# A graph layer on one core: another split of the gathered rows between two DMA queues, and one transfer for two groups

## The chip, the core and the metric

The kernel runs on one core of a Trainium2 chip. A core has a matrix engine (TensorE, PE in the profile), a vector engine (VectorE, DVE), an activation engine (ScalarE, ACT), a general engine (GpSimd, POOL) and a small engine that only waits and issues (SyncE, SP). DMA transfers are issued by SyncE, ScalarE and GpSimd and are carried out by DMA engines beside them. An issue is an instruction of the issuing engine, in order with its others; in the profile such instructions stand under SPq and ACTq and are not counted as busy time. The metric is the time of one execution in microseconds (us), as the device measures it.

## The reference

The layer has 6250 nodes with 128 features and 206250 edges, sorted by receiver. Cut to what matters:

```python
w = silu(edge_attr_32 @ rad_W1 + rad_b1) @ rad_W2 + rad_b2
w = w + silu(edge_attr_32_n2 @ sph_W1 + sph_b1) @ sph_W2 + sph_b2      # 206250 x 128
q = (x @ Wq)[receivers];  k = (x @ Wk)[senders];  v = (x @ Wv)[senders]
alpha = (q * w * k).reshape(-1, 8, 16).sum(-1) / 4 * edge_weight[:, None]
out = segment_sum(alpha[..., None] * v.reshape(-1, 8, 16), receivers, 6250) / 16
return layernorm(x + out.reshape(-1, 128))
```

## The kernel before

**Tiling.** A tile is 128 edges. Four tiles make a quad (512 edges) and four quads a group (2048 edges); there are 403 quads in 101 groups. Because the edges are sorted by receiver, the receivers of a quad lie in a window of 32 nodes.

**Startup (to about 90 us).** TensorE makes a table `kv_tab` in DRAM with k and v of every node, 1 KB a node. The receivers of all edges, relative to the start of their quad's window (`rel`), are transposed in tiles of 128 x 128 (`turn_rel`), stored to DRAM in `rel_lin` (L484) and spread from there to `rel_four`, four copies a quad (L489), so that a later load can put a quad's row of receivers on many partitions. This is done in two steps: `first_rel` for the first tile, and `store_rel(1, ...)` for the rest.

**The main loop** goes over the quads in a fixed order (in a group 0, 2, 1, 3; `slot` is the place in that order), with every instruction's place written out by hand. Iteration i does, for quads near i: on TensorE the group sums, the first layers of quad i+2 (L566), the queries at the edges of quad i+1 (L585) and its second layers (L618); on ScalarE the two silus of quad i+2 (L603) with copies between them; on GpSimd the gathers of quad i+14 from `kv_tab` (L142), one indirect DMA a tile of 128 edges; on VectorE the product of queries and keys (L634, `multiply`), the scores (L642, L644, L647) and messages (L659). The last matmul of L585 gives the one signal of TensorE in an iteration. The silus, the multiply and the next gathers wait for it.

**Row tiles.** GpSimd does not gather everything. In 58 of the quads, spread evenly (`row_at`), the fourth tile of 128 edges is fetched by 128 single DMAs of one row of 1 KB each (L212, tile `wide`); such a quad has three gathers and not four. Each row needs its address in a register. SyncE and ScalarE share these rows: ScalarE issues the last `ROW_ACT = 68`, SyncE the first 60. The registers are loaded from `at_i` by a load for up to 32 rows on SyncE and 24 on ScalarE (L206). `load_rows(i)`, at the end of each iteration, hands both engines their due part of the rows by a planner: a row costs 1, a register load `ROW_LOAD = 6`, and tile k is to be issued evenly over the 6.776 iterations that end six quads (`ROW_LEAD`) before the quad that uses it. ScalarE may put one row ahead of its copies and one behind (`next_rows` in `copies`); the rest comes behind its second silu. VectorE waits for the rows and the gathers of a quad at L631, just ahead of its multiply.

**What else SyncE issues, per group:** the node features x of a group (L315, at slot 0, for g+3), the receivers `relb` (L263, at slot 2, for g+3), the edge features `feats` (L252, at slot 3, for g+3) and the finished output (L777, at slot 1). x and feats are issued behind a wait for a signal of TensorE (`past`). SyncE works through all of it in program order.

The few lines that matter most:

```python
n = P - ROW_ACT
row_open.append({SP: rows_by(nc.sync, SP, 0, n), ACT: rows_by(nc.scalar, ACT, n, P)})
...
if slot == 3 and g + 3 < NG:
    load_feats(g + 3, past)
if slot == 2 and g + 3 < NG:
    load_rel(g + 3, lp, 4)
...
load_rows(i)
```

Of the kernel before, what the change touches and what calls it, by code (L numbers as in the profile page):

```python
# [12 lines left out]
F32 = mybir.dt.float32  # L13
BF16 = mybir.dt.bfloat16
# [7 lines left out]
SP = mybir.EngineType.SP  # L22
ACT = mybir.EngineType.Activation
WAIT = mybir.DependencyInfo(mybir.DependencyClass.Sync, mybir.DependencyReason.DATA)

P = 128
# [6 lines left out]
GT = 16  # L33
QT = 4
NQ = GT // QT
NG = math.ceil(E / (P * GT))
NT = NG * GT
EG = P * GT
EQ = P * QT
QUADS = math.ceil(E / EQ)  # L40
NB = math.ceil(N / P)
NBC = 7
ROWS = (NB + 1) * P
W = 32
# [7 lines left out]
ROW_FIRST = 8  # L52
ROW_LAST = 401
ROW_LEAD = 6
ROW_ACT = 68
ROW_AT = {SP: 0, ACT: 64}
ROW_LOAD = 6
ROW_CARRY = 2
ROW_UNITS = {SP: 32, ACT: 24}
# [14 lines left out]
def gnn_kernel(ctx, tc, x, src, dst, weight, edges, rad_W1, rad_b1, rad_W2, rad_b2,  # L74
# [14 lines left out]
    nc = tc.nc  # L89
    const = ctx.enter_context(tc.tile_pool(name="const", bufs=1))  # L90
    dram = ctx.enter_context(tc.tile_pool(name="dram", bufs=1, space=DRAM))

    kv_tab = dram.tile([NB * P, 2 * D], F32, name="kv_tab")
    rel_lin = dram.tile([NT, P], BF16, name="rel_lin")
    rel_four = dram.tile([NT // QT, NQ, EQ], BF16, name="rel_four")
    acc = dram.tile([ROWS, D], F32, name="acc")

    wkv = const.tile([P, 2 * D], F32, name="wkv")
# [29 lines left out]
    gp = ctx.enter_context(tc.tile_pool(name="group", bufs=2))  # L128
# [18 lines left out]

    order = [g * NQ + j for g in range(NG) for j in (0, 2, 1, 3) if g * NQ + j < QUADS]
    row_at = [ROW_FIRST + (n + 1) * (ROW_LAST - ROW_FIRST) // ROW_TILES for n in range(ROW_TILES)]
# [25 lines left out]
    feats_of, relb_of, act_of, kv_of, hot_of, hotT_of, x_of, q_of, msg_of = ({} for _ in range(9))  # L175
# [71 lines left out]
            return [(t, kv_of[q][:, t, :])]  # L247
        return [(slice(0, QT - 1), kv_of[q][:, :QT - 1, :]), (slice(QT - 1, QT), row_of[q])]

    def load_feats(g, mark=None):  # L250
        feats_of[g] = gp.tile([P, EG // 2], F32, name="feats", bufs=3)
        o = nc.sync.dma_start(feats_of[g], edges[g])  # L252
        if mark is not None:
            tc.add_manual_dep(o.ins, mark.ins.name, WAIT, reason="one signal of TensorE a quad")

    def quads_in(g):
        return min(NQ, QUADS - g * NQ)

    def load_rel(g, pool, bufs):

        relb_of[g] = pool.tile([P, EQ], BF16, name="relb", bufs=bufs)
        r = rel_four[g * NQ:(g + 1) * NQ].rearrange("j n e -> (j n) e")
        nc.sync.dma_start(relb_of[g], r[:, None, :].to_broadcast([NQ * NQ, W // NQ, EQ]))  # L263

    made = []

# [72 lines left out]
    with tc.tile_pool(name="nodes", bufs=1) as nodes, \  # L339
# [54 lines left out]
        relT = nodes.tile([P, math.ceil(NT / P), P], BF16, name="relT")  # L394
# [82 lines left out]
            nc.tensor.transpose(pt[:n, 0, :], rel[:, t:t + n], ident)  # L477
            nc.scalar.activation(relT[:n, t // P, :], pt[:n, 0, :], AF.Copy)

        def store_rel(a, b):  # L480
            for i, n in ((slice(a, min(b, NT // P)), P), (slice(NT // P, b), NT % P)):
                if i.start < i.stop:
                    t = slice(i.start * P, i.start * P + (i.stop - i.start) * n)
                    nc.sync.dma_start(rel_lin[t, :].rearrange("(n p) e -> p n e", p=n), relT[:n, i, :])  # L484
            a, b = a * P // QT, min(b * P, NT) // QT
            r = rel_lin.rearrange("(q t) e -> q (t e)", t=QT)
            for a, b in ((a, b - b % (P // 8)), (b - b % (P // 8), b)):
                if a < b:
                    nc.sync.dma_start(rel_four[a:b], r[a:b, None, :].to_broadcast([b - a, NQ, EQ]))  # L489

        def first_rel():
            turn_rel(0)
# [11 lines left out]
        n = len(chunks)  # L504
# [18 lines left out]
        for i, (k, n) in enumerate(work):  # L523
            if i + 2 < len(work):
                turn(*work[i + 2])
            kvs = k_and_v(k, n)
            for o, w in smalls[i:i + 1]:
                nc.scalar.dma_start(o, w)
            if i in behind:
                gather_x(behind[i], mark_of[k])  # L530
            if i >= len(chunks):
                kv_of[k[0]] = kvs
                a, b = ((j - len(chunks)) * (math.ceil(NT / P) - 1) // XQ for j in (i, i + 1))
                for t in range(a + 1, b + 1):
                    turn_rel(t * P)
                for f in beside.get(i, []):
                    f()
                continue
            store(k, kvs)
            if k + 8 < len(chunks):  # L540
                load_nodes(k + 8)
            if k == 4:
                nc.sync.dma_start(src_i, src)
            for f in beside.get(k, []):
                f()
            if i == len(chunks) - 1:
                load_rel(0, gp, 1)
                load_feats(0)
                for g in range(1, XL):
                    load_x(g)  # L550
                    load_feats(g)
                nc.sync.dma_start(scale, weight)
        for n, q in enumerate(order[XQ:AHEAD]):
            gathers(q, mark_of[quads_x[min(n + 2, XQ - 1)], "x"] if n else None)
        nc.vector.tensor_tensor(bsum, b2[:, 0:1], b2[:, 1:2], op=OP.add)
        store_rel(1, math.ceil(NT / P))
        nc.vector.tensor_scalar(scale, scale, SCALE, None, op0=OP.mult)


    with tc.tile_pool(name="ps", bufs=1, space=PSUM) as pp, tc.tile_pool(name="loop", bufs=1) as lp:  # L560
# [239 lines left out]
            nc.vector.tensor_scalar(general, found, 0.0, None, op0=OP.is_gt)  # L800

        written, ready, ready_at = [], [], []
        load_rel(1, lp, 4)
        load_rel(2, lp, 4)
        silus(order[0], first_layers(order[0]))
        pick(1)
        q_at_edges(order[0])
# [2 lines left out]
        mark = weigh(order[0])  # L810
        seen = [mark] * 3
        for g in range(NG - 1):
            for slot, j in enumerate((0, 2, 1, 3)):
                q = g * NQ + j
                i = g * NQ + slot
                turned, past, last = None, seen[-2], seen[-1]
                if slot == 0 and g == CHECK + len(checks) + 1:
                    verdict()
                if slot == 0:
                    turned = turn_q(g + 1, pp.tile([P, EQ], F32, name="pq", bufs=2))  # L820
                if slot == 1 and 2 <= g:
                    turned = sum_group(g - 2)
                if slot == 2:
                    turned = make_q(g + 1, pp.tile([P, EQ], F32, name="pq", bufs=2))
                if 1 <= g:
                    for t in ((), (0, 1), (2,), (3,))[slot]:
                        mark = sum_quads(g - 1, t)
                first_layers(order[i + 2])
                mark = q_at_edges(order[i + 1])
                seen.append(mark)  # L830
                weigh(order[i + 1])

                def copies():
                    next_rows(ACT, 1, loads=False)
                    if turned:
                        turned()
                    if 1 <= g and slot == 3:
                        part_sums(g - 1)
                    next_rows(ACT, 1, loads=False)

                silus(order[i + 2], mark, copies)
                if ready and ready_at[-1] <= i:
                    scaled(*ready.pop(0), i)
                if i + AHEAD < len(order):
                    gathers(order[i + AHEAD], last)
                multiply(order[i + 1], mark)
                messages(q, scores(q))
                if slot == 0:
                    if g + XL < NG:
                        load_x(g + XL, past)  # L850
                if slot == 3 and g + 3 < NG:
                    load_feats(g + 3, past)
                if slot == 2 and g + 3 < NG:
                    load_rel(g + 3, lp, 4)
                if slot == 0 and 1 <= g:
                    one_hots(g)
                if slot == 1:
                    one_hots_T(g + 1)
                    if g + 2 < NG:
                        pick(g + 2)  # L860
                if slot == (2 if g < NG - 2 else 0) and 1 <= g:
                    place(g - 1)
                if slot == 1:
                    write_rows(1, i)
                if slot == (3 if g < NG - 2 else 2):
                    if 2 <= g:
                        statistics(g - 2)
                if slot == 3:
                    if CHECK <= g < CHECK + len(checks):
                        checks[g - CHECK]()  # L870
                if g == NG - 4 and slot == 0:
                    place(NG - 2)
                if g == NG - 4 and slot == 1:
                    wide_one_hots(order[-1])
                if g == NG - 4 and slot == 3:
                    place(NG - 1)
                if g == NG - 3 and slot in (0, 2):
                    wide_one_hots(order[slot // 2 - 3])
                if g == NG - 2 and slot == 0:
                    n = nc.values_load(general, min_val=0, max_val=1)  # L880
                if g == NG - 3 and slot in (1, 3):
                    weigh_wide(order[slot // 2 - 3])
                if g == NG - 2 and slot == 1:
                    weigh_wide(order[-1])
                load_rows(i)
        g, (a, b, c) = NG - 1, order[-3:]
        first_layers(c)
        mark = q_at_edges(b)
# [41 lines left out]
        mark = q_at_edges(c)  # L930
# [196 lines left out]
```

## Time and profile before

| | |
|---|---|
| median of 3 runs | 2572.93 us (2570.8 to 2580.83) |
| the profiled execution's own time | 2581.4 us |
| its span (first to last instruction) | 2579.6 us |
| TensorE matmul, weight load | 2090.3 us (81%), 1743.4 us (68%) |
| VectorE, ScalarE, GpSimd busy | 1527.9 us (59%), 644.5 us (25%), 1474.3 us (57%) |
| granted TensorE clock | 0.844 |
| DMA | 307.15 MB, 119 GB/s |

The profile is one execution. In a timeline row stand the start and the length in us, the engine, the line, the operation, what it writes and reads, how many instructions are merged in the row, and in brackets how long the engine was idle before and what ended that. In the view of waits a row gives who waited at which line, for whom, the total in us, how many times, and the longest. In the view of stretches a row gives the stretch and its length in us, the busy time of an engine with the count of its instructions, and at the end the granted clock, the DMA engines' busy share and GB/s. "Remote" is a release that the profile puts down to no instruction it shows.

### The profile page before, as it was taken

The page shows a single profiled execution, that of the slowest core. Times are in us where ns is not written, and L with a number is a line of the kernel's source. Part 1 is how long each engine was busy: PE and PEld are TensorE (multiplying, and loading weights), DVE is VectorE, ACT ScalarE, POOL GpSimd, SP SyncE. Part 2 cuts the span into 40 slices and gives each one's busy share as a digit, 9 for nine tenths or more (in the row PEclk, how much of TensorE's full clock was granted, in tenths as well). Part 3 has the DMA queues.
Part 4 walks back from the last instruction along what each step waited for, and adds up shares of the span by engine and source line. Part 5 has one row for each costly group of instructions (what it writes and reads, how often), then busy time and mean ns, then how long its engine had stood idle before and what let it go on. Part 6 is the DMA issues. An engine that isn't in the chain of part 4 may idle for free.

```text
span 2579.6 us, 56198 instructions
## 1 busy us (share of the span) xinstructions
PE 2090.3 (81%) x16002; PEld 1743.4 (68%) x16002; DVE 1527.9 (59%) x3423; ACT 644.5 (25%) x1361; POOL 1474.3 (57%) x1562
## 2 busy tenths in 40 slices
PE   7687888888887878778788788888788888888788
PEld 6566766676666666667667676667566666666677
DVE  5465665656665655555556556556556555566568
ACT  2122222222222222222222222222222222222224
POOL 5565655656565556556566556556565555565550
PEclk8688888878888888888888888878888887888889
DMA  7433434344343434333343433334343443333331
GB/s 272 130 120 105 122 113 124 113 121 122 114 121 114 121 116 122 111 117 113 117 122 114 122 113 121 118 110 124 105 121 114 120 122 110 117 115 121 118 108 38
DMA packets 156799, 307.15 MB, mean 119 GB/s; under 512 B 41798, under 2 KB 90880, under 8 KB 156480
## 3 DMA queue, kind: packets, MB, share of 16 engines
q0 software_dynamic: 74080, 201.69, 27.0%
q1 hardware_dynamic: 72736, 97.22, 11.4%
q10 hardware_dynamic: 9664, 4.58, 0.7%
q8 instruction: 127, 2.08, 0.3%
q14 instruction: 192, 1.57, 0.2%
HBM read 289.88 MB, written 15.11 MB: 118 GB/s over the span
## 4 chain that ended last, share of the span: by engine, by line
PE 33%; issue 20%; DVE 15%; SPq 13%; another core or an unknown queue 12%; ACTq 5%; ACT 1%; DMA 1%; DVEq 0%
PE pw L618 14%; SPq L212 10%; PE pq L585 6%; PE ph L566 5%; ACTq L212 4%; DVE kq L634 3%; DVE side L644 3%; PE po L670 3%; DVE kq L642 3%; SPq L206 2%; PE pk L383 1%; ACTq L206 1%; PE pq L711 1%; DVE side L647 1%
## 5 line engine op out<-in xcount | busy, mean ns | idle before, releaser
L142 POOL DMA_INDIRECT kv<-kv_tab,src_i x1522 | 1442.9, 948 | 1017.6 <-remote 527.7
L618 PE MATMUL pw<-w,act 128*128 128x128 f32 x6448 | 1061.3, 323 | 131.5 <-issue 129.6
L618 PEld LDWEIGHTS pw<-w,act 128*128 128x128 f32 x6448 | 946.4, 229 | 214.3 <-issue 176.5
L603 ACT ACTIVATE act<-ph,b 128x512 f32<-128x512 f32 x806 | 554.6, 689 | 1856.5 <-remote 1559.2
L634 DVE TENSOR_TENSOR kq<-pq,kv 128x512 f32<-128x512 f32 (+1 forms) x404 | 271.1, 671 | 943.8 <-remote 765.7
L566 PE MATMUL ph<-feats,w 32*128 32x512 f32 x1612 | 673.5, 745 | 150.8 <-issue 143.1
L585 PE MATMUL pq<-q,hotT 32*128 32x128 f32 x3224 | 557.1, 321 | 10.0 <-DVE kq L634 6.8
L585 PEld LDWEIGHTS pq<-q,hotT 32*128 32x128 f32 x3224 | 470.8, 220 | 17.0 <-issue 16.7
L566 PEld LDWEIGHTS ph<-feats,w 32*128 32x128 f32 x1612 | 193.2, 209 | 317.4 <-issue 292.0
L644 DVE TENSOR_REDUCE side<-kq 128x32 f32<-128x512 f32 x404 | 280.2, 694 | 14.0
L659 DVE TENSOR_TENSOR msg<-kv,side 128x512 f32<-128x512 f32 (+1 forms) x404 | 269.0, 666 | 13.8
L642 DVE TENSOR_TENSOR kq<-pw,kq 128x512 f32<-128x512 f32 x404 | 274.5, 679 | 0.4 <-PE pw L618 0.4
L670 PE MATMUL po<-msg,hot 128*32 128x128 f32 x3200 | 183.2, 310 | 38.0 <-issue 37.7
L573 PE MATMUL pw<-brow,onesb 3*128 3x512 bf16 x403 | 176.6, 438 | 0.0
L670 PEld LDWEIGHTS po<-msg,hot 128*32 128x32 f32 x3200 | 86.5, 118 | 94.8 <-issue 67.4
L711 PE MATMUL pq<-part,to 128*128 128x128 f32 x196 | 58.4, 389 | 110.3 <-issue 76.1
L711 PEld LDWEIGHTS pq<-part,to 128*128 128x128 f32 x196 | 38.6, 246 | 126.4 <-issue 98.9
L647 DVE TENSOR_TENSOR side<-side,scale 128x32 f32<-128x32 f32 x400 | 79.8, 199 | 13.7
L292 DVE TENSOR_TENSOR hotT<-relb,side 128x512 f32<-128x512 bf16 x101 | 68.7, 680 | 0.0
L297 DVE TENSOR_TENSOR hot<-rel,side 128x512 f32<-128x512 f32 x100 | 68.0, 680 | 0.0
L286 PE MATMUL pq<-wq,xT 128*128 128x128 f32 x200 | 48.8, 331 | 10.0 <-DVE kq L634 7.7
L383 PE MATMUL pk<-wkv,xT 128*128 128x256 f32 x162 | 43.6, 412 | 13.1 <-DVE kv L385 10.0
(132 smaller groups left out, 851.6 us busy)
## 6 DMA issues: line engine op xcount, KB each, us to landing
wide<-kv_tab ACTq DMA_DIRECT2D x3944, 1.0 KB
wide<-kv_tab SPq DMA_DIRECT2D x3480, 1.0 KB
feats<-in_edges SPq DMA_DIRECT2D x101, 512.0 KB
kv<-kv_tab,src_i POOLq DMA_INDIRECT x1522, 2.8
relb<-rel_four SPq DMA_DIRECT2D x101, 128.0 KB
x<-in_x SPq DMA_DIRECT2D x101, 64.0 KB
out<-y SPq DMA_DIRECT2D x101, 64.0 KB
kv_tab<-kv SPq DMA_DIRECT2D x12, 512.0 KB
```

Source lines behind the costliest of these rows:

```text
L142: return nc.gpsimd.indirect_dma_start(out=o, out_offset=None, in_=table, in_offset=bass.IndirectOffsetOnAxis(ap=index, axis=0))
L212: o = engine.dma_start(row_of[q][p:p + 1, 0, :].bitcast(U8), table[:, ds(regs.pop(p), ROW_BYTES)])
L566: return nc.tensor.matmul(act_of[q, i], w1[r0:r0 + R, :], feats_of[g][r0:r0 + R, c0:c0 + EQ], start=True, stop=True)
L573: nc.tensor.matmul(pw, onesb[f:f + 3, :], brow[f:f + 3].rearrange("p t d -> p (t d)"), start=True, stop=False)
L585: o = nc.tensor.matmul(pq_of[q][:, t, :], hotT_of[g][b, t * P:(t + 1) * P], q_of[g][b, :], start=True, stop=True)
L603: o = nc.scalar.activation(act, act_of[q, i], AF.Silu, bias=b1[:, i:i + 1])
L618: o = nc.tensor.matmul(pw[:, t, :], act_of[q, i][:, t * P:(t + 1) * P], w2[:, i, :], start=False, stop=(t == QT - 1 and i == 1))
L634: o = nc.vector.tensor_tensor(kq_of[q][:, u, :], pq_of[q][:, u, :], kv[:, :, :D], op=OP.mult)
L642: nc.vector.tensor_tensor(m, pw_of[q][:, t, :], m, op=OP.mult)
L644: nc.vector.tensor_reduce(alpha, m.rearrange("p t (h e) -> p t h e", e=HD), AX.X, OP.add)
L659: nc.vector.tensor_tensor(msg_of[q][:, u, :].rearrange("p t (h e) -> p t h e", e=HD), kv[:, :, D:].rearrange("p t (h e) -> p t h e", e=HD) ...
L670: o = nc.tensor.matmul(po_of[g][j * W:(j + 1) * W, :], hot_of[g][:, j * QT + t, :], msg_of[g * NQ + j][:, t, :], start=(t == 0), stop=(t = ...
```

## The change

ScalarE issues the last 72 of a tile's 128 rows and SyncE the first 56. The addresses of ScalarE's rows move to column 56 of `at_i`. Edge features and receivers are loaded for two groups (a pair) by one transfer; it is issued in odd groups, at the same slots as before, and holds groups g+3 and g+4. Features have two buffers of a pair, where they had three of a group, and receivers two of a pair (and one for the first), where they had four of a group (and one). So that the receivers of a pair lie side by side in DRAM, `rel_lin` and `rel_four` get another layout (`rel_pair`), and `store_rel` writes it with stores of 16 partitions, two for each of four residues of the pair's number, and with spreads that are separate for the two groups of a pair. The first of these calls stores pair 0 alone.

```diff
+PAIRS = math.ceil(NG / 2)
-ROW_ACT = 68
-ROW_AT = {SP: 0, ACT: 64}
+ROW_ACT = 72
+ROW_AT = {SP: 0, ACT: 56}
-    rel_lin = dram.tile([NT, P], BF16, name="rel_lin")
-    rel_four = dram.tile([NT // QT, NQ, EQ], BF16, name="rel_four")
+    rel_lin = dram.tile([2, PAIRS, GT, P], BF16, name="rel_lin")
+    rel_pair = dram.tile([PAIRS, NQ, NQ, 2, EQ], BF16, name="rel_pair")
...
-    def load_feats(g, mark=None):
-        feats_of[g] = gp.tile([P, EG // 2], F32, name="feats", bufs=3)
-        o = nc.sync.dma_start(feats_of[g], edges[g])
+    def pair_of(u):
+        return range(2 * u, min(2 * u + 2, NG))
+
+    def load_feats(u, mark=None):
+        pair = pair_of(u)
+        feats = gp.tile([P, 2, EG // 2], F32, name="feats")
+        for g in pair:
+            feats_of[g] = feats[:, g - pair[0], :]
+        o = nc.sync.dma_start(feats[:, :len(pair), :],
+                              edges[pair[0]:pair[-1] + 1].rearrange("g p e -> p g e"))
...
-    def load_rel(g, pool, bufs):
-        relb_of[g] = pool.tile([P, EQ], BF16, name="relb", bufs=bufs)
-        r = rel_four[g * NQ:(g + 1) * NQ].rearrange("j n e -> (j n) e")
-        nc.sync.dma_start(relb_of[g], r[:, None, :].to_broadcast([NQ * NQ, W // NQ, EQ]))
+    def load_rel(u, pool, bufs):
+        pair = pair_of(u)
+        n = len(pair) * EQ
+        relb = pool.tile([P, 2 * EQ], BF16, name="relb", bufs=bufs)
+        for g in pair:
+            relb_of[g] = relb[:, (g - pair[0]) * EQ:(g - pair[0] + 1) * EQ]
+        r = rel_pair[u].rearrange("j n h e -> (j n) (h e)")[:, :n]
+        nc.sync.dma_start(relb[:, :n], r[:, None, :].to_broadcast([NQ * NQ, W // NQ, n]))
...
-        def store_rel(a, b):
-            for i, n in ((slice(a, min(b, NT // P)), P), (slice(NT // P, b), NT % P)):
-                if i.start < i.stop:
-                    t = slice(i.start * P, i.start * P + (i.stop - i.start) * n)
-                    nc.sync.dma_start(rel_lin[t, :].rearrange("(n p) e -> p n e", p=n), relT[:n, i, :])
-            a, b = a * P // QT, min(b * P, NT) // QT
-            r = rel_lin.rearrange("(q t) e -> q (t e)", t=QT)
-            for a, b in ((a, b - b % (P // 8)), (b - b % (P // 8), b)):
-                if a < b:
-                    nc.sync.dma_start(rel_four[a:b], r[a:b, None, :].to_broadcast([b - a, NQ, EQ]))
+        def store_rel(c, d):
+            ends_at = [min(d, (NG + 1 - h) // 2) for h in range(2)]
+            for u in range(c, min(c + NQ, d)):
+                for h, e in enumerate(ends_at):
+                    p, n = u % NQ * 2 * GT + h * GT, len(range(u, e, NQ))
+                    nc.sync.dma_start(
+                        rel_lin[h, u:e:NQ].rearrange("n m e -> m n e"),
+                        relT[p:p + GT, u // NQ:u // NQ + n, :])
+            for h, e in enumerate(ends_at):
+                r = rel_lin[h].rearrange("u (j t) e -> (u j) (t e)", t=QT)
+                m = e - (e - c) % NQ
+                for x, y in ((c, m), (m, e)):
+                    if x < y:
+                        nc.sync.dma_start(
+                            rel_pair[x:y, :, :, h, :].rearrange("u j n e -> (u j) n e"),
+                            r[x * NQ:y * NQ, None, :].to_broadcast([(y - x) * NQ, NQ, EQ]))
...
                 load_feats(0)
                 for g in range(1, XL):
                     load_x(g)
-                    load_feats(g)
+                load_feats(1)
...
-        store_rel(1, math.ceil(NT / P))
+        store_rel(1, PAIRS)
...
-        load_rel(1, lp, 4)
-        load_rel(2, lp, 4)
+        load_rel(1, lp, 2)
...
-                if slot == 3 and g + 3 < NG:
-                    load_feats(g + 3, past)
-                if slot == 2 and g + 3 < NG:
-                    load_rel(g + 3, lp, 4)
+                if slot == 3 and g % 2 == 1 and g + 3 < NG:
+                    load_feats((g + 3) // 2, past)
+                if slot == 2 and g % 2 == 1 and g + 3 < NG:
+                    load_rel((g + 3) // 2, lp, 2)
```

## The prediction

> **What bounds the kernel now.** I read the page first, then the waits of VectorE (DVE) and of SyncE's queue (SPq) in two stretches, then the pace in the same stretches, then the timeline around one stall. The page names no single bound, and its busy shares count no DMA issue, so the engine that this change touches, SyncE, does not appear in them. Its issues do:
>
> ```profile
> wide<-kv_tab ACTq DMA_DIRECT2D x3944, 1.0 KB
> wide<-kv_tab SPq DMA_DIRECT2D x3480, 1.0 KB
> feats<-in_edges SPq DMA_DIRECT2D x101, 512.0 KB
> relb<-rel_four SPq DMA_DIRECT2D x101, 128.0 KB
> ```
>
> Row tiles: 58 x 68 rows by ScalarE (ACT) and 58 x 60 by SyncE. The view of waits for VectorE, first from 200 to 1015 us, then from 1015 to 2480:
>
> ```profile
> DVE kq L634 <- remote: 276.0, 110, 5.7
> DVE kq L634 <- PE pq L585: 26.3, 13, 5.6
> DVE kq L634 <- DVEq L631: 2.1, 1, 2.1
> ...
> DVE kq L634 <- remote: 436.3, 173, 2.9
> DVE kq L634 <- DVEq L631: 66.4, 16, 9.7
> DVE kq L634 <- PE pq L585: 46.3, 27, 2.9
> DVE kq L634 <- DMA wide<-kv_tab: 20.4, 4, 7.1
> ```
>
> L631 is VectorE's wait for a quad's gathered rows, L634 the multiply behind it. Up to 1015 us it costs 2.1 us; afterwards 66.4 + 20.4 = 86.8 us in 20 waits. The rows come late only in the second part. Why, the waits of SyncE's own queue tell, from 200 to 1015 us (one line) and from 1015 to 2480:
>
> ```profile
> SPq L315 <- remote: 0.5, 3, 0.2
> ...
> SPq L315 <- DVE y L732: 0.7, 1, 0.7
> SPq L315 <- PE pq L585: 0.4, 2, 0.2
> SPq L315 <- DVE h L759: 0.3, 1, 0.3
> SPq L252 <- remote: 0.2, 1, 0.2
> ```
>
> 1.6 us of waiting in 1465: SyncE is never ahead of anything; it issues without pause, in the first part too (0.5 us of waits in 815). It falls behind slowly, uses up the lead that the schedule gives it (ROW_LEAD, six quads), and from about 1015 us each tile's multiply waits for SyncE's last row. One such wait in the timeline:
>
> ```profile
> 1090.19 6.28 SPq L212 DMA_DIRECT2D wide<-kv_tab  x11
> ...
> 1096.47 0.37 SPq L263 DMA_DIRECT2D relb<-rel_four  x1
> 1097.29 3.17 SPq L212 DMA_DIRECT2D wide<-kv_tab  x8
> 1102.00 0.56 DVE L634 TENSOR_TENSOR kq<-pq,kv 128x384 f32<-128x384 f32 x1 [9.68 <-DVEq L631]
> ...
> 1102.82 0.36 SPq L252 DMA_DIRECT2D feats<-in_edges  x1
> ```
>
> The row issues end at 1100.46 and the multiply starts 1.5 us later. ScalarE's rows of the same tile are not what is late; its issues keep finishing inside the iteration (below). The price of the late rows is read from the pace. The reduce L644 runs once a quad; its count in two stretches that begin and end at a row tile's multiply, before and after the lead is gone:
>
> ```profile
> 310.60:973.00 662.40, 75.06 (x108) 0.86 0.40 118
> 973.00:2499.10 1526.10, 169.58 (x244) 0.84 0.39 117
> ```
>
> 662.4/108 = 6.133 us a quad, then 1526.1/244 = 6.255. So late rows cost (6.255 - 6.133) x 244 = 29.7 us net; the 86.8 us of waits are mostly won back in the next iterations. What sets 6.133 is another loop, which this change leaves alone: one iteration's gathers on POOL,
>
> ```profile
> 1082.43 0.95 POOL L142 DMA_INDIRECT kv<-kv_tab,src_i  x1 [1.46 <-remote]
> 1083.68 0.95 POOL L142 DMA_INDIRECT kv<-kv_tab,src_i  x1 [0.31 <-issue]
> 1084.93 0.94 POOL L142 DMA_INDIRECT kv<-kv_tab,src_i  x1 [0.30 <-issue]
> 1086.18 0.95 POOL L142 DMA_INDIRECT kv<-kv_tab,src_i  x1 [0.30 <-issue]
> 1088.55 0.69 DVE L634 TENSOR_TENSOR kq<-pq,kv 128x512 f32<-128x512 f32 x1 [2.79 <-remote]
> ```
>
> four at 1.25 us and then about 1.4 us until the signal of the next iteration, 6.3 in all; with three gathers it is 4.9 (1052.13 to 1057.01, in the rows of ScalarE below).
>
> **The change part by part.** *SyncE loses 4 rows a tile.* Their price: 6.28/11 = 0.57 us and 3.17/8 = 0.40 in the rows above; 0.57 is the commoner. Four are 1.6 to 2.3 us a tile; I take 2.2.
>
> *Features and receivers once in two groups.* A tile spans 393/58 = 6.776 quads, 1.69 groups, so 1.69 of the 3.39 such issues go. From the rows above each holds SyncE from its start to the next group's start: 1097.29 - 1096.47 = 0.8 us for receivers; the rows show 0.36 us at least. 1.69 x 0.36 to 0.8 = 0.6 to 1.4 us a tile; I take 1.0. The register loads stay at two a tile on SyncE (32 + 28 rows become 32 + 24) and three on ScalarE (24 + 24 + 20 become 3 x 24).
>
> What is needed: SyncE now takes 6.776 x 6.255 = 42.4 us a tile and the other loop 6.776 x 6.133 = 41.6. It must lose 0.8 us; it loses 3.2, and even the low ends (1.6 + 0.6) suffice by more than two. So SyncE gets ahead, its lead stays near the full six quads, and it begins to wait for TensorE at load_x and load_feats. What is late next is nothing in the rows: the gather loop at 6.133. Gain: 29.7 us. The lower bound of the gain is 0 (SyncE's stalls could fill the freed time); the upper is the 86.8 us of waits, were none of them won back. The pace counts what is won back, so 29.7.
>
> *ScalarE gains 4 rows a tile*, 0.6 a quad. Two iterations, one with four gathers and one with three:
>
> ```profile
> 1083.63 2.78 ACTq L212 DMA_DIRECT2D wide<-kv_tab  x9
> 1088.55 0.69 ACT L603 ACTIVATE act<-ph,b 128x512 f32<-128x512 f32 x1 [4.54 <-remote]
> ...
> 1052.13 0.69 ACT L603 ACTIVATE act<-ph,b 128x512 f32<-128x512 f32 x1 [4.85 <-remote]
> ...
> 1053.14 3.70 ACTq L212 DMA_DIRECT2D wide<-kv_tab  x10
> 1057.01 0.69 ACT L603 ACTIVATE act<-ph,b 128x512 f32<-128x512 f32 x1 [3.25 <-PE pq L585]
> ```
>
> 2.78/9 = 0.31 and 3.70/10 = 0.37 us a row. In the first ScalarE is done at 1086.41, 2.1 us before its next silu is released: 0.2 us more is covered. In the second it is done at 1056.84, 0.17 us before: one more row (0.37) makes the silu 0.2 us late. Behind it wait TensorE's next first layers (they need the silu's bank). There are 58 short iterations: 58 x 0.2 = 12 us if all are hit and nothing absorbs it, 0 if the gathers end last anyway. With 0.6 row a quad and the gathers setting the signal, I take 3. If the cover in the long iterations were gone too, 57 tiles x 4 x 0.37 = 84 us is the far end.
>
> *Transfers of twice the size.* Features go from 512 KB to 1 MB at once. The stretch in which one of them runs, and the one before:
>
> ```profile
> 1020.00:1023.50 3.50, 2.83 (x24) 2.00 (x25) 2.97 (x7) 1.43 (x3) 2.23 (x3) 1.00 0.22 73
> 1023.50:1026.50 3.00, 1.78 (x16) 1.58 (x15) 0.48 (x2) 0.00 (x0) 1.56 (x2) 1.00 0.89 269
> ```
>
> The DMA engines are 89% busy for some 3 us; now 6 us, half as often. Rows and gathers issued meanwhile land up to 3 us later. Gathers are issued 14 quads ahead (86 us), rows with a lead of six: hidden, 0. With the lead gone (as now) it would count. The load is needed no earlier than before: it is issued at slot 3 of an odd group g for g+3 and g+4, as g+3 is now. The bytes are the same.
>
> *Startup.* The receivers' bounce through DRAM:
>
> ```profile
> 84.80 1.09 SPq L484 DMA_DIRECT2D rel_lin<-relT  x2
> 88.94 1.49 SPq L489 DMA_DIRECT2D rel_four<-rel_lin  x2
> 90.53 1.26 SPq L263 DMA_DIRECT2D relb<-rel_four  x2
> 97.07 0.37 SPq L315 DMA_DIRECT2D x<-in_x  x1
> ...
> 105.86 0.34 SPq L252 DMA_DIRECT2D feats<-in_edges  x1
> ```
>
> Two stores and two spreads become eight and four: 8 more at 0.5 to 0.75 us, 4 to 6 us on SyncE, and the next receivers (pair 1) now wait until the spread has landed. Cover: SyncE waits for TensorE's signals until 97.07 and 105.86 anyway, and groups 0 and 1 are already loaded by the first transfer. 0; bound +6, the whole delay. One group's features more at the start: bound 3 us, taken as 0.
>
> **Sum.** -29.7 + 3 + 0 + 0 = -26.7 us against the profiled execution's 2581.4 us: 2554.7. That execution lies 8.5 us above the median of the runs, 2572.93; carried over, 2546.
>
> **A rule against it.** The Trainium skill, page "DMA: Bandwidth & Descriptors", section "Issuing engines are not separate DMA queues", says that starting DMAs from more engines only saves the sequencer's time to start them, "which is usually small relative to the DMA itself". By that the change is worth nothing, 2573. The trace differs: SyncE's waits above are 1.6 us in 1465, so its issue time is the thing that is short, whatever its transfers take.
>
> **Rivals.**
> 1. *The relief does not arrive* (2573). SyncE's price per row is not fixed: 0.40 us in one group, 0.57 in another. If the price is a share of elapsed time (SyncE being held while gathers are issued), the rows left could stretch; or the profiler itself holds SyncE, and without it there is nothing to win. Against: 3.2 us are freed where 0.8 is needed, and profiled and plain times differ by 0.3% only.
> 2. *ScalarE becomes the bound* (slower). Its silus are in the loop of every quad. At 0.37 us a row, 57 x 4 rows on the path are +84 us: 2573 - 30 + 84 = 2627. It decides from 0.07 us of lateness a quad on average (30 us / 403); one extra row in the short iterations gives 0.03. For it: 0.17 us of slack in the short iteration. Against: 2.1 us in the long, which are 345 of 403.
> 3. *More than the pace shows* (2525). In the first part, too, iterations may lose something to a pressed SyncE; if rows on time win another 0.05 us a quad, 20 us more. Against: from 200 to 1015 us VectorE lost 2.1 us to rows.
>
> **Chances.** Forecast 0.68; rival 1 (with the skill's rule) 0.15; rival 2 0.09; rival 3 0.08. Faster by over 0.5% (13 us, about what a measurement of this kernel can tell from no change): 0.68 + 0.08 = 0.76; same 0.15; slower 0.09. The range: up to 2576 takes in rival 1 with the scatter of its runs, down to 2528 most of rival 3's way; outside lie rival 2 and the tails, under 2 in 10. The forecast's own range, from its terms (gain 22 to 40, ScalarE 0 to 12), is 2533 to 2563.
>
> **What would show it.** Right: VectorE's waits for L631 and for wide under 10 us; SyncE waits for PE or "remote" at load_x and load_feats, 100 us or more in all; 244 quads between row tiles in about 1496 us; 51 issues of features with 1024 KB. Wrong: SyncE's waits still near zero (rival 1); or ScalarE's silus starting later than VectorE's multiply of the same signal, with a pace above 6.2 (rival 2); or waits of TensorE or VectorE for feats or relb, which I put at nothing.

## The result, and the profile after

The changed kernel took 2544.89 us (median of 4 runs, 2538.09 to 2546.95), the kernel before 2576.88 us beside it (median of 4). The ratio is 0.9866, with a 95% interval from 0.984 to 0.9891: faster by 1.3%. The profiled execution took 2544.0 us, its span 2542.2 us. The forecast was 2546. That it came within 1 us is in part luck: the gain is 32 us where 27 were forecast, and the kernel before took 4 us more beside it than the median that the forecast started from.

The line numbers of the changed kernel differ: the wait for rows is L650 (before L631), the multiply L653 (L634), the reduce L663 (L644), the load of x L327 (L315), of edge features L259 (L252), the row issue L213 (L212). The issues, from the page (the last, half-filled transfer of features and of receivers stands apart there):

```profile
wide<-kv_tab ACTq DMA_DIRECT2D x4176, 1.0 KB
wide<-kv_tab SPq DMA_DIRECT2D x3248, 1.0 KB
feats<-in_edges SPq DMA_DIRECT2D x50, 1024.0 KB
...
relb<-rel_pair SPq DMA_DIRECT2D x50, 256.0 KB
```

VectorE's waits, from 200 to 1015 us and from 1015 to 2440 us:

```profile
DVE kq L653 <- remote: 253.4, 104, 5.3
DVE kq L653 <- PE pq L604: 49.0, 23, 3.2
...
DVE kq L653 <- remote: 478.1, 196, 3.0
DVE kq L653 <- PE pq L604: 58.1, 28, 5.1
```

The waits for rows, 86.8 us before, are gone: no row of L650 or wide is left. SyncE's own queue, from 1015 to 2440 us, now waits at the loads of x and of features, which are issued behind a signal of TensorE, as a queue that is ahead does:

```profile
SPq L327 <- remote: 34.3, 22, 4.0
SPq L259 <- remote: 17.1, 9, 3.7
SPq L259 <- PE pq L604: 10.5, 7, 4.0
SPq L327 <- PE pq L604: 3.1, 3, 1.7
```

That is 65 us, where it was 1.6; from 200 to 1015 us it is another 37, in all 102 (forecast: 100 or more). The pace, in the stretches between the same row tiles as in the prediction (a reduce a quad):

```profile
307.70:970.10 662.40, 75.06 (x108) 0.83 0.40 120
970.10:2462.80 1492.70, 169.58 (x244) 0.85 0.40 119
```

6.133 us a quad in the first stretch, exactly as before, and 6.118 in the second, where it was 6.255. Most of the gain lies in the second stretch: 1526.1 - 1492.7 = 33.4 us of the 37.4 us between the two profiled executions; 2.9 us lie ahead of the first stretch and 1.1 behind the second. The granted clock does not make this difference: the changed kernel has 6.133 at 0.83 in its first stretch, the kernel before 6.255 at 0.84. From the last row issue of SyncE for a tile to that tile's multiply there were 32 us at the first tile, 0.9 at the twenty-first and 1 to 6 from there to the last but one in the kernel before; in the changed kernel there are 30 to 38 us at all tiles but one.

### The profile page after: what moved, and what is told of

Same layout as the page of the kernel before. It is cut to its first block, busy times and chain, and to the rows that moved or that the text cites. A ratio compares the mean times of both kernels' runs of the same rounds, so it can differ in the third digit from the quotient of the medians.

```text
span 2542.2 us, 55993 instructions
## 1 busy us (share of the span) xinstructions
PE 2084.9 (82%) x16002; PEld 1742.8 (69%) x16002; DVE 1528.3 (60%) x3423; ACT 642.3 (25%) x1361; POOL 1470.8 (58%) x1562
## 4 chain that ended last, share of the span: by engine, by line
PE 47%; DVE 18%; issue 15%; another core or an unknown queue 14%; ACTq 5%; ACT 1%; DMA 0%; DVEq 0%; SPq 0%
PE pw L637 22%; PE pq L604 8%; PE ph L585 8%; ACTq L213 4%; PE po L689 4%; DVE kq L653 4%; DVE side L663 4%; DVE kq L661 3%; PE pq L730 1%; PE pk L395 1%; DVE side L666 1%; DVE msg L678 1%; DVE hotT L304 1%; ACTq L207 1%
## 5 line engine op out<-in xcount | busy, mean ns | idle before, releaser
L653 DVE TENSOR_TENSOR kq<-pq,kv 128x512 f32<-128x512 f32 (+1 forms) x404 | 271.0, 671 | 907.7 <-remote 787.5
L663 DVE TENSOR_REDUCE side<-kq 128x32 f32<-128x512 f32 x404 | 280.2, 694 | 14.0
L289 PE MATMUL pq<-pick,x 128*128 128x128 f32 x200 | 45.8, 311 | 6.6 <-issue 6.6
```

The costliest lines, as they stand in the source:

```text
L653: o = nc.vector.tensor_tensor(kq_of[q][:, u, :], pq_of[q][:, u, :], kv[:, :, :D], op=OP.mult)
L663: nc.vector.tensor_reduce(alpha, m.rearrange("p t (h e) -> p t h e", e=HD), AX.X, OP.add)
```

## The experiments

These runs came from two kinds of chip, two chips of each kind. On the one kind (below: the slower chip) the kernel before takes about 2570 us, as in the profile that the prediction read; on the other (the faster chip) about 1965. What sets them apart is not known. Each ratio below is to the kernel before on the same chip.

| run | edit | us | before | ratio, 95% interval |
|---|---|---|---|---|
| e1_split_only | split 72/56 alone | 2548.8 | 2571.33 | 0.9899, 0.988 to 0.9918 |
| e2_pairs_only | transfers for two groups alone | 2549.54 | 2571.33 | 0.9907, 0.9888 to 0.9926 |
| e5_sp_lead12 | before, SyncE's rows twelve quads ahead | 2585.73 | 2571.33 | 1.0046, 1.0027 to 1.0065 |
| e6_tiles40 | changed kernel, 40 row tiles | 2546.05 | 2571.33 | 0.9899, 0.9878 to 0.992 |
| f1_after_again | the changed kernel | 2538.49 | 2574.19 | 0.9864, 0.9845 to 0.9884 |
| f2_after_third | the changed kernel | 1964.19 | 1964.36 | 0.9998, 0.9984 to 1.0012 |
| e3_act80 | split 80/48 | 2111.87 | 1966.63 | 1.0736, 1.0722 to 1.075 |
| f3_act80_again | the same again | 2110.73 | 1964.36 | 1.0741, 1.0726 to 1.0756 |
| e8_tiles49 | 49 row tiles | 1975.56 | 1966.63 | 1.0049, 1.0036 to 1.0063 |
| e9_t40_act104 | 40 row tiles, split 104/24 | 1985.41 | 1966.63 | 1.0095, 1.0082 to 1.0108 |
| f4_t40_act104_again | the same again | 1985.33 | 1964.36 | 1.0103, 1.0089 to 1.0117 |
| e10_t40_act40 | 40 row tiles, split 40/88 | 1989.13 | 1966.63 | 1.0113, 1.01 to 1.0126 |

### One part alone

e1 is the kernel before with

```diff
-ROW_ACT = 68
-ROW_AT = {SP: 0, ACT: 64}
+ROW_ACT = 72
+ROW_AT = {SP: 0, ACT: 56}
```

> The kernel before with the new split alone (72 rows by ScalarE, 56 by SyncE), features and receivers still once a group. Theory (SyncE's issue time was short by 0.8 us a tile; four rows are 2.2 us): the whole gain comes already, 2542 to 2552 us, VectorE's waits for rows (L631 and wide) under 10 us, SyncE's queue waits for TensorE some 50 us in all. Rival (the larger transfers are what helped): 2565 to 2575 us, with 60 us or more of waits for rows left.

e2 is the changed kernel with the same two lines put back.

> The changed kernel with the old split (68 by ScalarE, 60 by SyncE): only the transfers for two groups are new. Theory: 1.0 us a tile is freed where 0.8 is short, so SyncE just keeps up: 2543 to 2558 us, waits for rows under 30 us, and next to no waiting by SyncE. So the two parts do not add up: each alone brings most of it. Rival (the split is the whole gain): 2570 us and 80 us of waits for rows.

Measured: 2548.8 and 2549.54 us, both as the theory expected. Each part alone brings 22 us, and both together 32 to 36: they do not add up, as two reliefs of one shortage do not. The pace of the second stretch, with the 244 quads of the same row tiles, shows it more sharply (e1, then e2):

```profile
974.10:2469.80 1495.70, 169.56 (x244) 0.85 0.39 119
...
971.00:2470.60 1499.60, 169.56 (x244) 0.85 0.40 119
```

6.130 and 6.146 us a quad, where it was 6.255 before and is 6.118 with both: the split alone brings 30.4 us of the 33.4, the transfers alone 26.5. How near to the edge each leaves SyncE, the waits tell. In e1 SyncE's queue waits a little for TensorE from 200 to 2440 us, 18 us in all and not the 50 that were expected, and VectorE never for rows:

```profile
SPq L252 <- remote: 9.4, 12, 3.1
SPq L315 <- remote: 7.0, 8, 2.5
```

In e2 VectorE still waits for rows, all of it from 1800 us on (the view is from 1015 to 2440 us):

```profile
DVE kq L653 <- DVEq L650: 11.7, 3, 5.0
...
DVE kq L653 <- DMA wide<-kv_tab: 8.4, 2, 5.0
```

There the time from SyncE's last row to the multiply, its lead, shrinks from 31 us at the first tile to 14 at the thirty-first and 0.3 at the fifty-first, by 0.6 us a tile. In the kernel before it shrank by 1.5 us a tile (32 to 0.9 in twenty tiles). So the transfers free about 0.9 us a tile where 1.5 was short, and SyncE just fails to keep up. The rival reading, that the larger transfers or the split alone is what helps, falls with both runs.

### More lead instead of fewer issues

e5 takes nothing away from SyncE. The planner of the kernel before reckons SyncE's due rows with a lead of its own (and `wide` has four buffers):

```diff
+ROW_LEAD_SP = 12
...
-        tiles = min(max((i - ROW_FIRST + ROW_LEAD) * ROW_TILES / (ROW_LAST - ROW_FIRST), 0), ROW_TILES)
+        tiles_of = {e: min(max((i - ROW_FIRST + lead) * ROW_TILES / (ROW_LAST - ROW_FIRST), 0), ROW_TILES)
+                    for e, lead in ((SP, ROW_LEAD_SP), (ACT, ROW_LEAD))}
```

> The kernel before, split and transfers unchanged, but the planner gives SyncE its rows twelve quads ahead and not six (ScalarE's stay at six; a fourth wide buffer). No instruction of SyncE is taken away. Theory: the loss comes from SyncE's lead running out after about 850 us, at 30 us in that time; 37 us more of lead last until after 1800 us, and what is lost then is at most a few us: 2545 to 2556 us, waits for rows under 25 us. Rival (the number of SyncE's issues itself slows the loop, by contention): 2570 to 2578 us.

Measured: 2585.73 us, slower by 0.5%. Both expectations missed. The rows were never late (from 1015 to 2440 us VectorE has no wait at the line that was L631), but SyncE is no less short, and what it issues late is now something else. TensorE's waits from 1015 to 2440 us:

```profile
PE ph L568 <- DMA feats<-in_edges: 70.0, 28, 5.2
```

L568 is the first layers. The features of group g+3 are issued behind iteration 4g+3 and needed in 4g+10, seven iterations or 43 us later. SyncE's issue of x, beside it, comes 38 us behind the multiply of its iteration in the second half of the run (median; 19 us in the kernel before, and 12 us ahead of it in the changed kernel): with earlier rows in front of them, the features arrive just too late, in 28 places. So the shortage is of SyncE's time, not of the rows' lead; a larger lead hands it to the next transfer in the same queue. That part of the theory stands, and my expectation failed because it gave the lead to the rows alone.

### Fewer rows

e6 tests the other half of the prediction, that with rows on time the gathers set the pace:

```diff
-ROW_TILES = 58
+ROW_TILES = 40
```

> The changed kernel with 40 row tiles and not 58: 18 more gathers on GpSimd, 2304 fewer row issues (1008 of them SyncE's). Theory (with rows on time the gather loop sets the pace, 6.3 us with four gathers and 4.9 with three): 18 x 1.3 to 1.4 = 23 to 25 us more than the changed kernel, 2567 to 2571 us. Rival (TensorE, or the pressed queues of SyncE and ScalarE, set the pace even now): no more than 2547 us, and less if the queues do.

Measured: 2546.05 us. The ratio is 0.9899 where the changed kernel has 0.9866 and 0.9864 (f1): about 8 us slower, with intervals that overlap, and not 23. The theory's range is missed, and the time lies in the rival's. The iterations still come in classes by their gathers, but all of them are shorter. The gathers of one iteration, and the first of the next:

```profile
1001.58 0.94 POOL L143 DMA_INDIRECT kv<-kv_tab,src_i  x1 [1.48 <-remote]
1002.83 0.95 POOL L143 DMA_INDIRECT kv<-kv_tab,src_i  x1 [0.30 <-issue]
1004.08 0.95 POOL L143 DMA_INDIRECT kv<-kv_tab,src_i  x1 [0.30 <-issue]
1005.33 0.95 POOL L143 DMA_INDIRECT kv<-kv_tab,src_i  x1 [0.30 <-issue]
```

Their spacing of 1.25 us is unchanged. The pause between one iteration's last gather and the next one's first, over all iterations from 200 to 2400 us, has a median of 1.60 us in the kernel before and the changed one (1.57 in f1) and of 1.50 here. What that is worth is read from the mean iteration: with four gathers 6.26 us here, 6.32 in the changed kernel and 6.29 in f1; with three 4.86, 4.95 and 4.92. Over 345 long and 58 short iterations this is 23 us beside the changed kernel's profile and 14 beside f1, against 22 us for the 18 gathers (18 x 1.25). So the gathers do enter the pace by their number (1.4 us lie between the two classes), but the rest of the loop is no constant: in this run, with fewer rows to issue for SyncE and ScalarE, it is shorter. Which engine's rows count, three more runs were to tell (e9 and e10 with another split of 40 tiles, e8 with 49 tiles), but they ran on the faster chip, where this pause does not exist. It stays open.

### The faster chip

e8, e9 and e10 differ from e6 and the changed kernel by these lines (the address columns of ScalarE's rows follow the split):

```diff
-ROW_TILES = 58
+ROW_TILES = 49     # e8, split 72/56
+ROW_TILES = 40     # e9, e10
-ROW_ACT = 72
+ROW_ACT = 104      # e9
+ROW_ACT = 40       # e10
```

> The changed kernel with 49 row tiles: 9 more gathers on GpSimd, 1152 fewer rows. If the time saved by fewer rows goes by their number, half way between 58 and 40 tiles, which are equal: 2540 to 2550 us. If the pause between the gathers jumps at some load of the queues, either 2533 us (the pause is short already) or 2557 us (it is still long).

> 40 row tiles, of whose rows ScalarE issues 104 and SyncE 24: as many rows by ScalarE (4160) as in the changed kernel with 58 tiles (4176), and 960 by SyncE. With 40 tiles split 72 and 56, the pause between two iterations' gathers was 1.50 us and with 58 tiles 1.60. If ScalarE's rows make that pause longer: back to 1.6 us, and 18 more gathers at 1.25 us are paid, 2562 to 2572 us. If it is SyncE's rows: 1.45 us or less, 2530 to 2545 us. If it is their sum: 1.50, 2541 to 2551 us.

> 40 row tiles, of whose rows ScalarE issues 40 (1600 in all) and SyncE 88 (3520, more than in the changed kernel's 3248). SyncE has 88 rows in 9.8 quads or 60 us, 0.57 us each: 50 us, so it keeps up. If SyncE's rows make the pause between the gathers longer: 1.6 us, 2562 to 2572 us. If ScalarE's: 1.4 us, 2520 to 2535 us. If their sum: 1.50, 2541 to 2551 us.

f4 is e9 once more:

> 40 row tiles, 104 rows by ScalarE and 24 by SyncE. Where the kernel before takes some 2570 us and the pause between two iterations' gathers was 1.60 us with 58 tiles and 1.50 with 40 split 72 and 56: if ScalarE's rows make the pause longer, 1.6 us and 2560 to 2570 us; if SyncE's rows do, 1.45 us or less and 2525 to 2542 us; if their sum, 1.50 us and 2542 to 2550 us. Where it takes 1967 us: 1985 us again.

Measured: 1975.56, 1985.41 and 1989.13 us beside 1966.63 for the kernel before, and 1985.33 for f4. The ranges of e8, e9 and e10 were made for the slower chip and say nothing here, so their questions stay open; f4 came out as expected for this chip. What these runs show is another bound. The changed kernel itself on the two chips:

> The changed kernel itself once more. Where the kernel before takes some 2570 us: 2536 to 2548 us again. Where it takes 1967 us (there GpSimd issues its gathers back to back, and 49 row tiles cost 9 us more, the price of 9 gathers): SyncE was not short there, so the same as before within 0.3%, 1960 to 1972 us; 40 us or more slower if ScalarE with its 72 rows a tile is already short there, as it is with 80.

> The changed kernel, once more beside the two below. Where the kernel before takes some 2570 us: 2535 to 2548 us. Where it takes 1967 us: SyncE is not short there and GpSimd's gathers are the bound, so no change, 1960 to 1972 us, unless ScalarE with 72 rows a tile is already short (1975 us and more).

f1 gave 2538.49 us and a ratio of 0.9864 on a slower chip. f2, on a faster one, gave 1964.19 us beside 1964.36: a ratio of 0.9998 with an interval of 0.14% to either side. Both are as expected. On the faster chip the change does nothing. Its timeline shows GpSimd (three of its gathers) and SyncE:

```profile
1002.00 0.95 POOL L143 DMA_INDIRECT kv<-kv_tab,src_i  x1 [0.30 <-issue]
...
1003.25 0.95 POOL L143 DMA_INDIRECT kv<-kv_tab,src_i  x1 [0.30 <-issue]
...
1004.50 0.95 POOL L143 DMA_INDIRECT kv<-kv_tab,src_i  x1 [0.30 <-issue]
```

```profile
1000.79 3.12 SPq L213 DMA_DIRECT2D wide<-kv_tab  x10
...
1014.14 3.20 SPq L213 DMA_DIRECT2D wide<-kv_tab  x10
```

The gathers follow each other at 1.25 us through the whole loop with no pause between iterations: 1522 x 1.25 = 1903 us of a span of 1962.6. GpSimd is the bound, and time goes by the gathers: 9 more cost 8.9 us and 18 more 19 to 22.5. SyncE's rows cost 0.31 to 0.32 us each there and not 0.57; with 60 rows it has 19 us of them in a tile of 6.776 x 4.72 = 32 us. With 56 rows, as here, its queue waits 304 us for TensorE from 200 to 1900 us:

```profile
SPq L327 <- PE pq L604: 194.1, 68, 8.0
SPq L259 <- PE pq L604: 109.8, 42, 6.7
```

It was not short, so there was nothing to free. (The kernel before was not profiled on that chip; that its SyncE had time to spare is worked out from these rows.)

e3 and f3 move three times as many rows to ScalarE as the change did, for rival 2:

```diff
-ROW_ACT = 72
+ROW_ACT = 80
```

> The changed kernel with 80 rows by ScalarE and 48 by SyncE. ScalarE gains 8 rows and a fourth register load a tile, 8 x 0.35 + 2.2 = 5 us a tile or 0.74 us a quad. Rival 2 (ScalarE is next to become the bound): its silus start late in a good part of the iterations and the time rises to 2555 to 2580 us. Theory that the gathers end last anyway: 2540 to 2550 us, the same as the changed kernel, with SyncE waiting much more.

> The changed kernel with 80 rows by ScalarE and 48 by SyncE, once more. Where the kernel before takes 1967 us: 2112 us again. Where it takes some 2570 us, an iteration is 6.1 us and not 4.7, and ScalarE has more room: 80 rows and 4 loads are 8 us of issues more a day of 41.5 than it can hide only in the short iterations, 2545 to 2565 us. If its issues were hidden wholly: 2535 to 2545 us.

Both runs of 80/48 fell on the faster chip: 2111.87 and 2110.73 us, 7.4% slower, which is more than either range of e3 allowed and what f3 expected. There ScalarE is the bound. The chain that ended last (f3; the view breaks the row off at its end):

```profile
by line: ACTq L213 49.6%; issue 15.0%; ACTq L207 12.3%; ACT act L622 5.2%; PE pw L637 3.0%; PE ph L585 2.5%; PE pq L604 1.7%; DVE kq L653 1.0%; DVE side L663 1.0%; PE pk L395 1.0%; DVE kq L661 0.9%; ACT y L765 0.4%; PE po L689 0.4%; ACT tot
```

ScalarE's row issues and register loads are 62% of it. 80 rows at 0.32 us and four loads at 1.8 are 33 us a tile, and a tile takes 6.776 x 5.08 = 34. With 72 rows and three loads it is 28, under the 32 that the gathers need. So rival 2 is real, eight rows away on that chip. On the slower one, where a tile takes 41.5 us, 80 rows were not measured.

## Why the prediction was right

**SyncE's time was short, and the rows late for it.** Right, on the slower chip. Less work for SyncE took the waits for rows away in one of two ways and most of them in the other (e1, e2), and a larger lead without less work did not help (e5). The gain from the pace, 29.7 us, came out at 33.4.

**What was short, 0.8 us a tile.** Misread, without harm to the sum. The 0.8 was taken from the second stretch, where the late rows already hold the loop back. While the lead lasted, SyncE's last rows came 43.2 us a tile apart and the multiplies 41.7 (the first twenty-one tiles): 1.5 us a tile. The 3.2 us of relief cover that too.

**The price of the parts.** About right, counted against the 1.5 us. The transfers, taken as 1.0 us a tile, free 0.9 (e2, above). The four rows, taken as 2.2, free about 1.8: with them alone the lead holds at 30 us for most of the run, and SyncE waits 18 us in 54 tiles, 0.3 a tile. Both together, taken as 3.2, free 3.4: the waits of 102 us in 54 tiles are 1.9 a tile. These are net sums: the rows left became a little dearer, on average 0.60 us from one to the next (0.59 in f1) where it was 0.57. Rival 1's mechanism is there in part, too weak to matter.

**ScalarE, taken as 3 us.** Its silu started later than the multiply of the same signal in 32 iterations, by 12 us in sum; 11 and 2.8 us before (counted in the two traces, iterations 12 to 384). That is the size of the upper bound, 12, yet the pace shows no loss at all: 6.118 where 6.133 was forecast. The term was at most that and was absorbed.

**Transfers of twice the size, and the startup, taken as 0.** Right: in the changed kernel neither VectorE nor TensorE waits for feats or relb in the loop, and the first multiply comes at 90.3 us (91.6 before).

**"That gather loop sets 6.133."** Half right. Gathers enter the pace by their number and are issued 1.25 us apart, on both chips. The 1.4 us from the end of the gathers to the next signal was treated as fixed; with fewer rows (e6) it fell by 0.1 us by the median (0.06 by the mean iteration with four), and on the faster chip the pause is not there.

**The rule of the Trainium skill, 2573.** On the slower chip it failed as the prediction said, because the sequencer's time was what was short; on the faster chip, where SyncE's was not, the rule's outcome is what was measured: no change. With 80 rows it fails there too: ScalarE's issues and register loads are what that run waits for (f3).

## What to carry to other kernels

An engine that only issues DMAs shows as idle on a page of busy shares; ask instead whether its queue ever waits, since a queue that waits for nothing may be the bound, and a lead in the schedule only hides this until the lead is used up. Read the pace of the same loop before and after that point: the difference, not the sum of the waits, is what the shortage costs. Part of the relief can bring most of the gain (here each half two thirds of the time, and 79 to 91% by the pace), and more lead without relief can just move the wait to the next transfer of that queue, as in e5.

## What the runs showed of the hardware that was not expected

The same program takes 2570 us on one chip and 1965 on another, and a change can be worth 1.3% on the one and nothing on the other. The granted clock, 0.846 and 0.955 in the profiled runs of the changed kernel, is not the whole of it: TensorE's busy time differs by 294 us, the span by 580. On the slower chip SyncE pays 0.4 to 0.7 us a row while GpSimd issues gathers, and a third of a microsecond as soon as it doesn't. In the kernel before, the last gather is issued at 2507.92 us; SyncE's rows ahead of it and behind it:

```profile
2480.01 6.24 SPq L212 DMA_DIRECT2D wide<-kv_tab  x9
...
2504.83 6.09 SPq L212 DMA_DIRECT2D wide<-kv_tab  x11
...
2524.58 3.51 SPq L212 DMA_DIRECT2D wide<-kv_tab  x11
...
2546.01 9.40 SPq L212 DMA_DIRECT2D wide<-kv_tab  x28
```

0.55 to 0.69 us a row in these, then 0.32 to 0.34. On the faster chip the rows cost 0.32 us beside gathers without a pause, and TensorE's signal does not wait for the gathers to end.

It is not the issue of a DMA alone that is held. Ahead of each row SyncE moves its address into place (`MOVE`). How long this took, in ns (least, median, longest), in the changed kernel on the slower and on the faster chip:

```profile
L213 SPq MOVE wide<-kv_tab x3248: 2/29/1412, 100.7 to 2495.7; - x192
...
L213 SPq MOVE wide<-kv_tab x3248: 29/29/38, 77.8 to 1910.6; - x192
```

TensorE is held as well: its matmuls started late by 332 us in sum from 200 to 2400 us with nothing that the profile shows to wait for; on the faster chip by 1.2 us from 200 to 1900. What holds the engines on the slower chip, no run here tells.
